# Layer 0 of a two-layer macaron block: who loads x, when the chains run, and how the attention's averages are spread over the next key tile

## The chip, the cores and the metric

The kernel runs on one core of one Trainium2 chip. The metric is the device time of one execution in microseconds; the time of a kernel is the median of its runs. The engines are TensorE (PE in the profile; its weight loads are PEld), VectorE (DVE), ScalarE (ACT), GpSimd (POOL) and SyncE (SP), whose queue issues most transfers. Each engine works through its own list of instructions in the order in which they stand there.

## The reference

Layer 0 works on x, 16 batches of 512 tokens with 128 features: half a quantized feed-forward network is added, then an attention with relative positions, then half a feed-forward network again. Layer 1 (mixture of experts and linear attention) follows and is not touched here.

```python
def _L0_attn_ref(x, W_qkv, b_qkv, W_out, b_out, rel_emb_k, rel_emb_v):
    ...
    dist = jnp.clip(idx[None, :] - idx[:, None], -R, R) + R      # R = 64
    pe_k = rel_emb_k[dist]
    pe_v = rel_emb_v[dist]
    ...
    score = jnp.einsum('bhqd,bhkd->bhqk', q, k) + jnp.einsum('bhqd,qkd->bhqk', q, pe_k)
    attn = jax.nn.softmax(score, axis=-1)
    ctx = jnp.einsum('bhqk,bhkd->bhqd', attn, v) + jnp.einsum('bhqk,qkd->bhqd', attn, pe_v)
    ctx = jnp.transpose(ctx, (0, 2, 1, 3)).reshape(b, s, d)
    return ctx @ W_out + b_out

def _L0_ffn_ref(x, w_gate, w_up, w_down):
    ...                                  # fp4_linear rounds both operands to 4 bits in blocks of 16
    gate = fp4_linear(x, w_gate)
    y = fp4_linear(x, w_up)
    h = jax.nn.silu(gate) * y
    return fp4_linear(h, w_down)
...
x = x + 0.5 * _L0_ffn_ref(_layernorm(x, axis=-1), ...)
x = x + _L0_attn_ref(_layernorm(x, axis=-1), ...)
x = x + 0.5 * _L0_ffn_ref(_layernorm(x, axis=-1), ...)
```

There are 16 heads of 8 features.

## The kernel before

The attention of layer 0 works in 32 units: a unit is half a batch, 256 queries, against all 512 keys of the batch in four key tiles of 128. A score is one PSUM tile of 128 keys by 32 queries of 16 heads: four matmuls of queries and keys (L263) and, where the distances are not clipped, eight more for the relative positions (L267). Every score is computed twice. The first time DVE takes its maximum over the keys (`maxima`, L341; per unit 32 scores, then a reduction `mk` at L347, a transpose on PE at L349, and the negated maxima go by way of MD in HBM into row 28 of the query tile a_BD). The second time the maximum is already in the operands, and ScalarE takes the exponential into PT (`main`, L369). Both kinds of scores share three PSUM buffers (`pS`). The maxima run about half a unit ahead of the exponentials.

With PT, PE computes the averages (`av`, 16 matmuls a key tile) and the band runs for the relative positions of the values (`rps`, 16 or 32 matmuls a run); `run` (L272 to L274) keeps the matmuls of such a run together. ScalarE copies the band sums to RV (L403) and the averages to cx (L412). RV goes to HBM (RD, L406) and comes back in another order (a_cr, L409); `fin` adds it (L422), divides, and applies the output weights (L430, L437, L440, L443).

Besides, there are chains of small steps: `head` is the first feed-forward half of a half batch, `tail` the last (both `FFN.half`: L55 statistics, L62, L116, L121, L123, L126, L133, L139, L140), `prep` makes queries and keys of a batch and writes them to HBM (QS, QM, KSd, L286 to L309), `prepV` the values. `loads` brings a_KS (L315), a_BD (L329) and a_TQ (L330) back for the maxima of a unit. `tail` ends with the store of the half batch (L486).

The tile of x of a batch lives from the load (L475) through head, prep, fin and tail to the second store. Its pool `xk` has five buffers, so batch b takes that of batch b-5. In the kernel before, `head` itself loads x, on SP's queue, when it begins.

`interleave` (L446) sets the order of the program: each generator has a number of steps n and a start f and an end t in units, and the one whose next step is due first goes on. A unit u starts at time u. `main` has 59 steps: eight scores of a key tile, then the averages and four empty steps, then the band runs of a finished half with empty steps. The numbers in W are the due times of the chains, counted from their unit; `pl` and `hl` say how many batches ahead prep and head run. The tile framework then places the instructions on each engine by a simulated timeline, in which this order is the priority, and adds the waits.

Of the kernel before, what the change touches and what calls it, by code (L numbers as in the profile page):

```python
# [8 lines left out]
F32 = mybir.dt.float32  # L9
# [136 lines left out]
class Attn0:  # L146
# [103 lines left out]
    @staticmethod  # L250
    def vers(kt,half):

        return 1 if kt*128+192<half*256+256 else 0
# [12 lines left out]
                w0=kt*128-blk*32-x+a.OFF  # L266
                nc.tensor.matmul(out[:,x*64:x*64+64],a.ET[:,w0:w0+128],TQ[:,:,b*32+4*x:b*32+4*x+4],start=False,stop=(x==7),skip_group_check=True)  # L267

    xnT={}; pend={}; last=None
    def run(a, mms):  # L270

        r=a.nc.tensor.matmul(*mms[0][0],**mms[0][1])  # L272
# [85 lines left out]
    def main(a, b, half, X, wk, big, pS, pA, pM):  # L358
        s=a.s; nc=a.nc; i=b%2
        u=(2*b+half)%3; BD=a.BD[u]; TQ=a.TQ[u]; KS=a.KS[b%2]; V=a.V[b%2]; RD=a.RD[half]; cr=a.cr[0]  # L360
        av=[pA.tile([128,512],F32,name=f"av{z}") for z in range(2)]
        RV=wk.tile([128,4,4,4,16],F32,name="RV")
        PT=[None]*4
        for kt in range(4):
            pt=big.tile([128,16,256],F32,name="PT"); PT[kt]=pt
            for bb in range(8):
                ps=pS.tile([128,512],F32,name="sps")
                a.scores(ps,kt,half,bb,BD,TQ,KS)
                nc.scalar.activation(pt[:,:,bb*32:bb*32+32].rearrange("p h (x j) -> p x h j",j=4),ps.rearrange("p (x h j) -> p x h j",x=8,j=4),AF.Exp)  # L369
                yield  # L370
            vs=a.vers(kt,half)
            mms=[]
            for z in range(4):
                for cg in range(4):
                    h=z*4+cg
                    o=av[z//2][cg*32:cg*32+32,(z%2)*256:(z%2)*256+256]
                    fs=(kt==0 and z%2==0)
                    mms.append(((o,V[:,2*kt-1+vs,h*9:h*9+32],pt[:,h,:]),dict(start=fs,stop=(kt==3),skip_group_check=True,tile_position=(0,cg*32))))
            a.run(mms)
            for _ in range(4): yield  # L380
            for hb in range(2):
                bl=range(hb*4,hb*4+4)
                ks=[k for k in range(4) if any(a.inband(k,half*8+x) for x in bl)]
                if max(ks)!=kt: continue
                rps=pA.tile([128,512],F32,name="rps")
                first=[True]*4
                mms=[]
                for b0 in bl[::2]:
                    ok=[(bb,k) for k in reversed(ks) for bb in (b0+1,b0) if a.inband(k,half*8+bb)]
                    for n,(bb,k) in enumerate(ok):  # L390
                        blk=half*8+bb
                        for x in range(8):
                            cg=x%4; col=(bb-hb*4)*128+(x//4)*64
                            v0=(blk*32-k*128+a.UO)//8
                            mms.append(((rps[cg*32:cg*32+32,col:col+64],a.TV[a.vers(k,half)][:,x,v0-8*a.vers(k,half):v0-8*a.vers(k,half)+4,:].rearrange("p v d -> p (v d)"),
                                PT[k][:,:,bb*32+4*x:bb*32+4*x+4]),
                                dict(start=first[cg],stop=(k==min(q for p,q in ok if p==bb)),skip_group_check=True,tile_position=(0,cg*32))))
                            first[cg]=False
                    a.run(mms); mms=[]
                    yield  # L400
                    yield
                for c in range(4):
                    nc.scalar.copy(RV[:,:,c,:,hb*8:hb*8+8].rearrange("p j z a -> p a z j"),rps.rearrange("p (a z c j) -> p c a z j",a=8,z=4,j=4)[:,c])  # L403
                yield

        nc.sync.dma_start(RD[:,:4*8*1024].rearrange("x (r f) -> x r f",f=1024),RV)  # L406
        for c in range(4):
            src=bass.AP(tensor=RD.tensor,offset=RD.offset+c*64,ap=[[1024,8],[8*1024+256,16],[1,64]])
            nc.sync.dma_start(cr[c*32:c*32+8].rearrange("p (xj f) -> p xj f",f=64),src)  # L409
        cx=wk.tile([128,4,256],F32,name="cx")  # L410
        for zz in range(2):
            nc.scalar.copy(cx[:,2*zz:2*zz+2,:].rearrange("p z (b j x) -> p (z b) x j",j=4,x=8),av[zz].rearrange("p (y x j) -> p y x j",x=8,j=4))  # L412
        a.pend[b,half]=cx,cr
        yield

    def fin(a, b, half, X, wk, pM):

# [28 lines left out]
def interleave(*gens):  # L446

    live=[[g,n,0,f,t] for g,n,f,t in (q if len(q)==4 else (*q,0,1) for q in gens)]
    while live:
        k=min(live,key=lambda r:r[3]+(r[4]-r[3])*r[2]/r[1])  # L450
        try: next(k[0]); k[2]+=1
        except StopIteration: live.remove(k)
# [4 lines left out]
def layer0(tc, s, w, src, dst, nb=16):  # L457
    nc=tc.nc
    tok=lambda x,b: x[b].rearrange("(t p) d -> p t d",p=128)
    P="L0_attn_"; names=["W_qkv","b_qkv","W_out","b_out","rel_emb_k","rel_emb_v"]  # L460
    with ExitStack() as c:
        s.const=c.enter_context(tc.tile_pool(name="c",bufs=1))
        pM=c.enter_context(tc.tile_pool(name="pM",bufs=2,space=PS))
        pF=c.enter_context(tc.tile_pool(name="pF",bufs=0,space=PS)) if 0 else pM
        pS=c.enter_context(tc.tile_pool(name="pS",bufs=3,space=PS))
        pX=pS
        pA=c.enter_context(tc.tile_pool(name="pA",bufs=1,space=PS))
        wk=c.enter_context(tc.tile_pool(name="wk",bufs=1))
        fk=c.enter_context(tc.tile_pool(name="fk",bufs=2))
        xk=c.enter_context(tc.tile_pool(name="xk",bufs=5))  # L470
        X={}
        def xload(b):
            if b in X or b>=nb: return
            t=xk.tile([128,4,128],F32,name="x"); X[b]=t
            nc.sync.dma_start(t,tok(src,b))  # L475
        def head(b,h):

            if b<nb: xload(b); yield from F.half(X[b],h,fk,pF)
        def prep(b):
            if b<nb: yield from A.prep(b,X[b],wk,pM)  # L480
        def prepV(b):
            if b<nb: yield from A.prepV(b,pM)
        def tail(b,h):
            if b<0: return
            yield from F.half(X[b],h,fk,pF)
            nc.sync.dma_start(tok(dst,b)[:,2*h:2*h+2,:],X[b][:,2*h:2*h+2,:])  # L486
        def mxs(b,half):
            if b>=nb: return
            yield from A.maxima(b,half,wk,pX,pM)
        def loads(u):  # L490
            if u<2*nb:
                if u%2==0: A.loadK(u//2)
                A.load(u//2,u%2)
        def stream():
            for u in range(1,2*nb):
                for k,_ in enumerate(mxs(u//2,u%2)):
                    if k==16: loads(u+1)
                    yield
        st=stream()
        def part(n):  # L500
            for _ in range(n):
                if next(st,0)==0: return
                yield
        pl,hl=2,3
        W=dict(part=0,V=(.6,.7),fin=(.45,.9),prep=(0,.7),tail=1.0,head=(-.1,1))
        with tc.tile_pool(name="wp",bufs=1) as wp:
            for b in range(3): xload(b)
            F=FFN(s,w["L0_ffn_w_gate"],w["L0_ffn_w_up"],w["L0_ffn_w_down"],wp,pF)
            ffn2=lambda f,b: interleave((f(b,0),21,0,.8),(f(b,1),21,.2,1))
            ffn2(head,0)  # L510
            A=Attn0(s,wp,pS,*[w[P+n] for n in names])
            def run(g):
                for _ in g: pass
            run(prep(0)); run(prepV(0)); loads(0); run(mxs(0,0))
            FFN1.pre(s,wp,[pA.tile([128,512],F32,name=f"av{z}") for z in range(2)]+[pA.tile([128,512],F32,name="rps")],w)
        big=c.enter_context(tc.tile_pool(name="big",bufs=3))
        loads(1); ffn2(head,1); run(prep(1)); run(part(14)); ffn2(head,2)
        S=[(part(99999),33*2*nb,W['part'],2*nb+W['part'])]
        for b in range(nb):
            for h in range(2):  # L520
                u=2*b+h
                def at(g,n,f,t): S.append((g,n,u+f,u+t))
                at(A.main(b,h,X,wk,big,pS,pA,pM),59,0,1)
                fn,tl=(W['fin'],W['tail']) if u<2*nb-2 else ((.3,.5),.6)
                at(A.fin(b,h,X,wk,pM),5,1+fn[0],1+fn[1])
                at(tail(b,h),21,1+fn[1]+.001,1+fn[1]+tl)
                if b+hl<nb: at(head(b+hl,h),21,*W['head'])
                if h==0 and b+pl<nb: at(prep(b+pl),11,*W['prep'])
                if h==1 and b+1<nb: at(prepV(b+1),1,*W['V'])
        interleave(*S)  # L530


# [249 lines left out]
class Attn1:  # L782
# [38 lines left out]
    X={}  # L821
# [216 lines left out]
```

## Time and profile before

| what | value |
|---|---|
| median of 3 runs | 3630.38 us (3630.13 to 3631.83) |
| profiled execution, its own time | 3633.94 us |
| its span | 3632.2 us |
| loop of layer 0 (first to last exponential) | 175.5 to 1974.5 us |
| PE busy, share of the span | 2825.0 us, 78% |
| DVE busy | 2444.9 us, 67% |
| ACT busy | 1693.8 us, 47% |
| POOL busy | 838.9 us, 23% |

The busy times are sums over stages with different limits, so the loop of layer 0 has to be read by itself. In listings of waits the columns are: the waiting engine, tile and line, what it waited for, the total in us, how many times, the longest in us. In listings in order of time they are start, duration, engine, line, operation, output from input, and in brackets the idle time before with what ended it. In tables of windows they are the stretch, its length, the busy time of PE, PEld, DVE, ACT and POOL with the number of instructions, the granted clock of PE as a share of full speed, the busy share of the DMA engines, and GB/s; a sum line adds up the stretches.

### The profile page before, as it was taken

How to read it: one execution, taken by the hardware profiler on the slowest of the kernel's cores; microseconds unless marked ns; L12 is line 12 of the kernel's file. 1: busy time of each engine (PE TensorE's matmuls, PEld its weight loads, DVE VectorE, ACT ScalarE, POOL GpSimd, SP SyncE). 2: the span in 40 equal slices, each digit the busy share in tenths (PEclk: the TensorE clock that was granted, in tenths of full speed). 3: DMA queues.
4: the chain of work that ended last, by engine and by line, in shares of the span. 5: the costliest groups of instructions: out<-in, count | busy, mean ns of one | idle time of the engine just before them, and what ended most of it. 6: DMA issues, size and time to landing. Idle time of an engine off the chain costs nothing. (4 is left out here: it accounts for less than half of the span.)

```text
span 3632.2 us, 95259 instructions
## 1 busy us (share of the span) xinstructions
PE 2825.0 (78%) x40077; PEld 2032.3 (56%) x40077; DVE 2444.9 (67%) x6508; ACT 1693.8 (47%) x3391; POOL 838.9 (23%) x789
## 2 busy tenths in 40 slices
PE   5578989889898889888896388873788888878570
PEld 3357777667676677666775244431565555555230
DVE  5568788777887788877773467774546655655356
ACT  3145555545455454545554155533455454445242
POOL 4122222222222222222110222212112211111226
PEclk8799999999999999999998599886899989989785
DMA  3232222321223222222210111104312222121401
GB/s 105 54 91 71 57 53 59 81 63 52 65 65 77 64 50 58 76 74 62 53 33 19 32 33 36 36 33 123 90 54 73 59 63 56 36 62 36 126 17 46
DMA packets 290159, 217.23 MB, mean 60 GB/s; under 512 B 77402, under 2 KB 257476, under 8 KB 289604
## 3 DMA queue, kind: packets, MB, share of 16 engines
q1 hardware_dynamic: 284468, 207.72, 21.6%
q8 instruction: 315, 5.16, 0.6%
q10 hardware_dynamic: 5264, 3.43, 0.4%
q14 instruction: 112, 0.92, 0.1%
HBM read 110.28 MB, written 100.78 MB: 58 GB/s over the span
## 5 line engine op out<-in xcount | busy, mean ns | idle before, releaser
L341 DVE TRANSPOSE_TENSOR_REDUCE mx<-sps 128x16 f32<-128x512 f32 x1024 | 702.5, 701 | 261.7 <-PE sps L263 137.2
L263 PE MATMUL sps<-a_BD,a_KS 128*128 128x128 f16 x8192 | 736.4, 222 | 136.2 <-DVE mx L341 65.6
L369 ACT ACTIVATE PT<-sps 128x512 f32<-128x512 f32 x1024 | 576.4, 599 | 433.8 <-PE sps L267 238.1
L263 PEld LDWEIGHTS <-a_KS 128*128 128x128 f16 x8192 | 546.1, 98 | 296.4 <-issue 260.0
L59 POOL TENSOR_TENSOR ln_rs<-ln_ve,negh 128x4 f32<-128x4 f32 (+1 forms) x192 | 176.9, 930 | 855.1 <-DVE ln_ve L58 760.6
L267 PE MATMUL sps<-a_TQ,a_ET 128*128 128x64 f16 x7168 | 370.3, 195 | 0.0
L721 DVE SCALAR_TENSOR_TENSOR moe<-mps,oh,moe 128x128 f32<-128x128 f32 x896 | 289.8, 341 | 110.7 <-PE mps L719 96.5
L79 POOL TENSOR_TENSOR q_M<-q_y,q_M 128x704 f32<-128x704 f32 (+2 forms) x129 | 157.0, 1218 | 784.6 <-DVE q_y L78 658.6
L719 PE MATMUL mps<-f_W,T 128*128 128x512 f32 x512 | 297.1, 701 | 24.8 <-DVE moe L721 20.0
L267 PEld LDWEIGHTS <-a_ET 128*128 128x128 f16 x7168 | 311.2, 99 | 2.3 <-issue 1.9
L274 PE MATMUL av<-PT,a_V 128*32 128x256 f32 x3840 | 251.9, 387 | 0.0
L894 DVE TENSOR_TENSOR a_at<-pp,a_cm 128x1024 f32<-128x1024 f32 x128 | 154.3, 1214 | 79.6 <-PE pp L892 78.6
L892 PE MATMUL pp<-a_F 64*128 64x128 f32 x2048 | 169.8, 306 | 41.4 <-DVE a_at L894 30.2
L892 PEld LDWEIGHTS pp<-a_F 64*128 64x128 f32 x2048 | 143.3, 206 | 93.0 <-DVE a_at L894 36.9
L719 PEld LDWEIGHTS mps<-f_W,T 128*128 128x128 f32 x512 | 102.7, 222 | 125.0 <-issue 75.3
L274 PEld LDWEIGHTS av<-PT,a_V 128*32 128x32 f32 x3840 | 121.4, 111 | 68.7 <-issue 5.0
L874 ACT ACTIVATE a_F<-pp 128x1024 f32<-128x1024 f32 x128 | 127.0, 1025 | 46.8 <-PE pp L872 40.5
L62 ACT ACTIVATE xn<-xn,ln_mr,ln_rs 128x128 f32<-128x128 f32 x256 | 103.6, 481 | 95.5 <-DVE ln_mr L60 75.2
L274 PE MATMUL rps<-PT,a_TV 128*32 128x64 f32 x6912 | 134.5, 222 | 4.6 <-issue 4.4
L139 PE MATMUL mps<-wdT,hT 128*128 128x128 f32 (+1 forms) x768 | 126.9, 301 | 5.6 <-ACT hT L136 4.0
L673 ACT COPY f_PT<-St 32x512 f32<-32x512 f32 x128 | 78.7, 615 | 106.0 <-DVE St L672 99.9
L872 PE MATMUL pp<-a_QK,a_PK 128*128 128x512 f16 x256 | 82.7, 413 | 54.4 <-DMA a_QK<-a1d 26.6
(342 smaller groups left out, 5330.2 us busy)
## 6 DMA issues: line engine op xcount, KB each, us to landing
QM<-a_HM SPq DMA_DIRECT2D x180, 128.0 KB
a_TQ<-QM SPq DMA_DIRECT2D x120, 192.0 KB
RD<-RV SPq DMA_DIRECT2D x32, 512.0 KB
a_KS<-KSd SPq DMA_DIRECT2D x128, 96.0 KB
a_QK<-a1d SPq DMA_DIRECT2D x128, 96.0 KB
xn<-X SPq DMA_DIRECT2D x32, 256.0 KB
a1d<-a_hi SPq DMA_DIRECT2D x64, 128.0 KB
a_BD<-QS SPq DMA_DIRECT2D x128, 58.0 KB
```

Source lines behind the costliest of these rows:

```text
L59: nc.gpsimd.tensor_tensor(rs,ve,s.negh[:,:n],ALU.pow); yield
L79: nc.gpsimd.tensor_tensor(M[:P],y[:P],M[:P],ALU.subtract)
L263: nc.tensor.matmul(o4[:,g],KS[:,sd,g*512+kt*128:g*512+(kt+1)*128],BD[:,g,:,b*32:b*32+32].rearrange("p h (x j) -> p x h j",j=4),start=(g==0 ...
L267: nc.tensor.matmul(out[:,x*64:x*64+64],a.ET[:,w0:w0+128],TQ[:,:,b*32+4*x:b*32+4*x+4],start=False,stop=(x==7),skip_group_check=True)
L274: for p,q in mms[1:]: a.nc.tensor.matmul(*p,**q)
L341: with a.s.tc.high_priority(): r=nc.vector.tensor_reduce(mx[:,kt,:,bb],ps.rearrange("p (i c) -> p i c",c=32),axis=AX.X,op=ALU.max,apply_tr ...
L369: nc.scalar.activation(pt[:,:,bb*32:bb*32+32].rearrange("p h (x j) -> p x h j",j=4),ps.rearrange("p (x h j) -> p x h j",x=8,j=4),AF.Exp)
L719: nc.tensor.matmul(ps,yT[:,j*128:(j+1)*128],a.W[:,e2*4:e2*4+4,:],start=True,stop=True)
L721: nc.vector.scalar_tensor_tensor(moe[:,j,:],ps[:,e*128:(e+1)*128],oh[:,j,e2*4+e:e2*4+e+1],moe[:,j,:],ALU.mult,ALU.add)
L874: nc.scalar.activation(f,ps,AF.Relu)
L892: nc.tensor.matmul(ps[:,hh,bs],f[hh*64:hh*64+64,1,bs],f[hh*64:hh*64+64,0,bs],start=True,stop=True)
L894: nc.vector.tensor_tensor(k,ps.rearrange("p h (b q) -> p (h b) q",b=4),a.cm.unsqueeze(1).to_broadcast([128,8,128]),ALU.mult)
```

## The change

The load of x leaves `head` and becomes a generator of its own, `xl`, issued on ScalarE's queue with a due time 1.3 to 1.4 units before the unit by which it is counted. Head runs two batches ahead instead of three, with later due times; fin, tail and prep are due later as well; the head of batch 2 moves from before the loop into it. `main` has 32 steps, one per score, with no empty ones: averages, band runs, copies and the end of a unit are put into a list `todo`, and after each exponential one portion of the list is issued. A unit's last portions run among the first scores of the next unit; `rest` issues what is left at the very end. The tiles av, rps and RV are allocated when the first portion needs them.

```diff
-    xnT={}; pend={}; last=None
+    xnT={}; pend={}; last=None; todo=[]
...
     def main(a, b, half, X, wk, big, pS, pA, pM):
...
+        def avrun(kt):
+            if kt==0: T["av"]=[pA.tile([128,512],F32,name=f"av{z}") for z in range(2)]
...
+            a.run(mms)
+        def rvrun(hb, b0, ks):
+            if b0%4==0: T["rps"]=pA.tile([128,512],F32,name="rps"); T["first"]=[True]*4
...
+            a.run(mms)
+        def rvcopy(hb):
+            if hb==0: T["RV"]=wk.tile([128,4,4,4,16],F32,name="RV")
+            for c in range(4):
+                nc.scalar.copy(T["RV"][:,:,c,:,hb*8:hb*8+8].rearrange("p j z a -> p a z j"),T["rps"].rearrange("p (a z c j) -> p c a z j",a=8,z=4,j=4)[:,c])
+        def end():
+            nc.sync.dma_start(RD[:,:4*8*1024].rearrange("x (r f) -> x r f",f=1024),T["RV"])
...
+            a.pend[b,half]=cx,cr
         for kt in range(4):
...
                 nc.scalar.activation(pt[:,:,bb*32:bb*32+32].rearrange("p h (x j) -> p x h j",j=4),ps.rearrange("p (x h j) -> p x h j",x=8,j=4),AF.Exp)
+                if a.todo: a.todo.pop(0)()
                 yield
-            a.run(mms)
-            for _ in range(4): yield
+            a.todo.append(lambda kt=kt: avrun(kt))
             for hb in range(2):
...
-                    a.run(mms); mms=[]
-                    yield
-                    yield
...
+                a.todo+=[lambda hb=hb,b0=b0,ks=ks: rvrun(hb,b0,ks) for b0 in bl[::2]]+[lambda hb=hb: rvcopy(hb)]
+            if kt==3: a.todo.append(end)
+    def rest(a):
+        while a.todo: a.todo.pop(0)(); yield
...
-        def xload(b):
-            if b in X or b>=nb: return
+        def xload(b, eng=nc.sync):
             t=xk.tile([128,4,128],F32,name="x"); X[b]=t
-            nc.sync.dma_start(t,tok(src,b))
+            eng.dma_start(t,tok(src,b))
+        def xl(b):
+            xload(b,nc.scalar); yield
         def head(b,h):
-            if b<nb: xload(b); yield from F.half(X[b],h,fk,pF)
+            if b<nb: yield from F.half(X[b],h,fk,pF)
...
-        pl,hl=2,3
-        W=dict(part=0,V=(.6,.7),fin=(.45,.9),prep=(0,.7),tail=1.0,head=(-.1,1))
+        pl,hl=2,2
+        W=dict(part=0,V=(.6,.7),fin=(.6,1.0),prep=(1.03,1.9),tail=1.0,head=(-1.05,0))
...
-        loads(1); ffn2(head,1); run(prep(1)); run(part(14)); ffn2(head,2)
+        loads(1); ffn2(head,1); run(prep(1)); run(part(14))
...
-                def at(g,n,f,t): S.append((g,n,u+f,u+t))
-                at(A.main(b,h,X,wk,big,pS,pA,pM),59,0,1)
+                def at(g,n,f,t): S.append((g,n,max(u+f,0),max(u+t,.5)))
+                at(A.main(b,h,X,wk,big,pS,pA,pM),32,0,1)
...
+                if h==0 and 2<b+hl<nb: at(xl(b+hl),1,-1.4,-1.3)
                 if b+hl<nb: at(head(b+hl,h),21,*W['head'])
...
+        S.append((A.rest(),8,2*nb,2*nb+.15))
         interleave(*S)
```

More of the change, by code (lines that the diff above doesn't have):

```diff
@@ L360, in main @@
         u=(2*b+half)%3; BD=a.BD[u]; TQ=a.TQ[u]; KS=a.KS[b%2]; V=a.V[b%2]; RD=a.RD[half]; cr=a.cr[0]
-        av=[pA.tile([128,512],F32,name=f"av{z}") for z in range(2)]
-        RV=wk.tile([128,4,4,4,16],F32,name="RV")
-        PT=[None]*4
+        PT=[None]*4; T={}; vers=a.vers
+        def avrun(kt):
+            if kt==0: T["av"]=[pA.tile([128,512],F32,name=f"av{z}") for z in range(2)]
+            vs=vers(kt,half)
+            mms=[]
+            for z in range(4):
+                for cg in range(4):
+                    h=z*4+cg
+                    o=T["av"][z//2][cg*32:cg*32+32,(z%2)*256:(z%2)*256+256]
+                    fs=(kt==0 and z%2==0)
+                    mms.append(((o,V[:,2*kt-1+vs,h*9:h*9+32],PT[kt][:,h,:]),dict(start=fs,stop=(kt==3),skip_group_check=True,tile_position=(0,cg*32))))
+            a.run(mms)
@@ new lines, in rvrun @@
+        def rvrun(hb, b0, ks):
+            if b0%4==0: T["rps"]=pA.tile([128,512],F32,name="rps"); T["first"]=[True]*4
+            rps=T["rps"]; first=T["first"]
+            mms=[]
+            ok=[(bb,k) for k in reversed(ks) for bb in (b0+1,b0) if a.inband(k,half*8+bb)]
+            for bb,k in ok:
+                blk=half*8+bb
+                for x in range(8):
+                    cg=x%4; col=(bb-hb*4)*128+(x//4)*64
+                    v0=(blk*32-k*128+a.UO)//8-8*vers(k,half)
+                    mms.append(((rps[cg*32:cg*32+32,col:col+64],a.TV[vers(k,half)][:,x,v0:v0+4,:].rearrange("p v d -> p (v d)"),
+                        PT[k][:,:,bb*32+4*x:bb*32+4*x+4]),
+                        dict(start=first[cg],stop=(k==min(q for p,q in ok if p==bb)),skip_group_check=True,tile_position=(0,cg*32))))
+                    first[cg]=False
+            a.run(mms)
@@ new lines, in rvcopy @@
+        def rvcopy(hb):
[4 more added lines that the diff above has]
+            nc.sync.dma_start(RD[:,:4*8*1024].rearrange("x (r f) -> x r f",f=1024),T["RV"])
+            for c in range(4):
+                src=bass.AP(tensor=RD.tensor,offset=RD.offset+c*64,ap=[[1024,8],[8*1024+256,16],[1,64]])
+                nc.sync.dma_start(cr[c*32:c*32+8].rearrange("p (xj f) -> p xj f",f=64),src)
+            cx=wk.tile([128,4,256],F32,name="cx")
+            for zz in range(2):
+                nc.scalar.copy(cx[:,2*zz:2*zz+2,:].rearrange("p z (b j x) -> p (z b) x j",j=4,x=8),T["av"][zz].rearrange("p (y x j) -> p y x j",x=8,j=4))
+            a.pend[b,half]=cx,cr
@@ L369, in main @@
                 nc.scalar.activation(pt[:,:,bb*32:bb*32+32].rearrange("p h (x j) -> p x h j",j=4),ps.rearrange("p (x h j) -> p x h j",x=8,j=4),AF.Exp)
+                if a.todo: a.todo.pop(0)()
                 yield
[L371 to L378, printed above, removed]
-            a.run(mms)
-            for _ in range(4): yield
+            a.todo.append(lambda kt=kt: avrun(kt))
             for hb in range(2):
@@ L384, in main @@
                 if max(ks)!=kt: continue
[L385 to L398, printed above, removed]
-                    a.run(mms); mms=[]
-                    yield
-                    yield
[L402 to L414, printed above, removed]
+                a.todo+=[lambda hb=hb,b0=b0,ks=ks: rvrun(hb,b0,ks) for b0 in bl[::2]]+[lambda hb=hb: rvcopy(hb)]
+            if kt==3: a.todo.append(end)
+    def rest(a):
+        while a.todo: a.todo.pop(0)(); yield
     def fin(a, b, half, X, wk, pM):
```

## The prediction

> **What bounds the kernel now.** I read the span by slices first, then stretches of it by engine, then who waited for whom, then the order of time around the longest waits. The attention loop of layer 0 runs from the first exponential at 175.5 us to 1975 us, half of the span; the rest is not touched. In the loop:
>
> ```profile
> core 0: us, PE busy (x) PEld busy (x) DVE busy (x) ACT busy (x) POOL busy (x), PEclk, DMA share, GB/s
> 1000.00:1200.00 200.00, 179.77 (x3154) 141.06 (x3152) 163.66 (x364) 105.20 (x232) 48.55 (x47) 0.97 0.26 66
> ```
>
> PE sets the pace: it is busy for 90% at a granted clock of 0.97, DVE for 82%. What can be won is PE's idle tenth and the clock. The list of waits, from 400 to 1800 us, and that of the SP queue, say where it goes:
>
> ```profile
> DVE ln_st L55 <- DMA x<-in_L_attn_x_dram: 45.5, 11, 5.2
> PE sps L263 <- DVE mx L341: 45.0, 53, 3.9
> PE sps L263 <- ACT PT L369: 27.1, 64, 2.6
> PE sps L349 <- DVE hq_sc L71: 9.9, 11, 0.9
> ```
> ```profile
> SPq L475 <- DMA X<-x: 28.8, 11, 3.4
> ```
>
> Eleven times, once per batch (each batch has two units), DVE stands still for a load of x that is issued when it is already needed. The load can't be issued earlier: SP holds it until the store of an older batch has left the buffer. The order of time at one of the eleven:
>
> ```profile
> 756.29 0.39 SPq L486 DMA_DIRECT2D X<-x  x1
> 760.14 0.39 SPq L475 DMA_DIRECT2D x<-in_L_attn_x_dram  x1
> 760.64 1.68 SPq L315 DMA_DIRECT2D a_KS<-KSd  x4
> ...
> 765.24 3.55 SPq L330 DMA_DIRECT2D a_TQ<-QM  x1
> ...
> 774.04 3.36 SPq L330 DMA_DIRECT2D a_TQ<-QM  x1
> 777.50 0.66 SPq L406 DMA_DIRECT2D RD<-RV  x1
> ```
> ```profile
> 763.46 1.07 DVE L55 BATCH_NORM_STATS2 ln_st<-x 128x6 f32<-128x128 f32 x5 [5.16 <-DMA x<-in_L_attn_x_dram]
> ```
> ```profile
> 766.07 0.59 PE L263 MATMUL sps<-a_BD,a_KS 128*128 128x128 f16 x4 [3.89 <-DVE mx L341]
> ```
>
> PE idles 3.89 us behind DVE. The same listing shows two more things for later: a store of x lands 3.5 us after its issue has ended (756.68 to 760.14), and from the last four a_KS loads to the instruction behind the last a_TQ load SP needs 16.9 us (760.64 to 777.50).
>
> **The change part by part.** Line numbers are those of the kernel before. *The wait for x goes.* The windows of 8 us that begin with DVE's eleven waits, and eleven windows of 80 us between them, sum to:
>
> ```profile
> sum 88.00, PE 55.06 PEld 41.12 DVE 42.69 ACT 33.64 POOL 14.82; mean PE 5.01 PEld 3.74 DVE 3.88 ACT 3.06 POOL 1.35
> ```
> ```profile
> sum 880.00, PE 792.97 PEld 603.74 DVE 749.94 ACT 446.38 POOL 201.69; mean PE 72.09 PEld 54.89 DVE 68.18 ACT 40.58 POOL 18.34
> ```
>
> PE idles 32.9 of 88 us around the waits and 9.9% elsewhere, which would be 8.7: 24 us are owed to x. Behind a wait the clock sinks too:
>
> ```profile
> 768.00:770.00 2.00, 2.00 (x29) 2.00 (x28) 2.00 (x7) 1.15 (x4) 0.00 (x0) 0.50 0.21 63
> 770.00:774.00 4.00, 4.00 (x99) 3.86 (x97) 3.16 (x14) 2.28 (x4) 1.10 (x1) 0.78 0.18 47
> ```
>
> With 766 to 768 also at 0.50 the worst wait lost 1.0 + 1.0 + 0.9 = 2.9 us of clock; I take half of that as the mean of the eleven, 16 us (bounds 0 and 32). In the changed program x is loaded about a unit before its first L55, so 24 + 16 = 40 us go (24 to 56).
>
> The Trainium skill speaks of the clock in "TensorE: Matmul & The Clock Gate", section "What's actually happening": half rate comes after about 3.4 us of idling. By that rule alone only the three or so waits over 3.4 us would cost clock, some 9 us by the row of the worst, and the part would be 33 us, not 40. The row decides.
>
> *ScalarE's queue gets the load, and with it the wait.* The load still needs its buffer, and so the store of an older batch. In the built order of the changed program the eleven loads that reuse a buffer (batches 5 to 15) stand in ScalarE's order directly behind the second exponential of units 4, 6, ... 24, and the two copies of L116 and the third exponential behind them. The store they wait for is the second of its batch; SP has it behind the a_KS loads and four pairs of a_BD and a_TQ. The last four a_KS wait for the last score of the unit before. What an engine does with a load that waits is shown at the start, where ScalarE issues some:
>
> ```profile
> 95.84 9.16 ACTq L330 DMA_DIRECT2D a_TQ<-QM  x8
> 105.04 0.37 ACT L116 COPY f_x<-mps 128x256 f32<-128x256 f32 x1 [17.45 <-DMA a_TQ<-QM]
> ```
> ```profile
> 105.47 1.54 PE L121 MATMUL mps<-wguT,f_x 128*128 128x352 f32 x2 [13.89 <-ACT f_x L116]
> ```
>
> It holds all that stands behind, here the same L116 and L121 as there. The price, counted from the last score of unit 2b-1: SP 16.9 us for the loads, 0.4 for the store's issue, 3.5 until it lands, 0.4 for the load's issue, 0.4 for L116: PE can go on with L121 at 21.6 us. Until then PE has, in its order: nine scores at 0.47 us (eight L267 follow four L263 by 0.23 us twice), L133 0.84, two L139 at 0.94, the averages 1.9, two band runs of 16 at 0.33, four L115 0.76: 10.3 us. Idle 11.3, less the 1 us that it would idle anyway in 10: 10.3 us, eleven times: 113. The clock costs what it did behind x, 16: +129. After such a stop DVE and ScalarE have no backlog, so the usual tenth is missing for some 10 us: 1 us each, -11. Bounds: where a_TQ is loaded for a second half batch, three of them go out in 1.34 us (at 700.59), 0.45 each and not 3.5; the quickest a_BD takes 0.26. With such rows SP needs 1.7 + 2.8 + 0.4 + 3.5 = 8.4 us, and PE does not stop at all: 0. With a store issue of 3.57 us (as at 714.26) it is 3.2 us more each: 129 + 35 = 164. I take 129, since all loads behind a_KS show the slow rows.
>
> In "DMA: Bandwidth & Descriptors", section "Issuing engines are not separate DMA queues", the skill says that issuing from another engine saves only the time of the issue. Here that would be 11 x 0.39 us on SP, 4 us, and the sum without both waits would lose the 40 us above as well; no row tells issue time from the wait it carries, so this is left at the rows.
>
> *Averages, band runs and copies, one portion per score.* The same instructions, none more. In the built order exponentials' scores and maxima's scores now alternate almost strictly, where before up to five of one kind follow each other, and each portion stands alone. Of PE's 45.0 + 27.1 us behind DVE and ScalarE 24 are x; the other 48 may halve: -24, for the whole loop -30. The chain waits of L437 and L440 (19.4 and 11.4 us before them) get a score or two more cover: -20. Against it L349, which waits 0.9 us for DVE in eleven units: it now stands one score behind the last maximum in even units, while the reduction (0.70) and both mk (1.06) have to run: about 1 us more in each of 31 units, +30. Together -20 (bounds -60 and +40).
>
> *Chains a unit later.* Preparing a batch now ends just before its loads: twelve QM issues (8.0 us on SP) stand ahead of MD and the a_BD row it feeds. From the order I count seven pairs of scores, 12 us, between that row and the next unit: 0; without that cover the first score would wait. RD goes behind the same slow loads: 16.9 + 0.4, then 9.6 until a_cr is issued (SP waits 9.6 at most for RD), 1.4 and some 2.5 to land: 31 us after the boundary, and its sum (L422) stands 19 pairs behind, about 34: 0. The head of batch 2 moves from before the loop into it, and so the last head a unit later: 6.5 us of PE work for each half, gone at the start and back at the end: 0 (10 either way).
>
> The sum, from the profiled execution's own 3633.9 (span 3632.2 and 1.7 around it): - 40 + 129 - 11 - 20 = 3692. The median of the runs is 3.6 lower: **3688 us**.
>
> **The rivals.** *The store lands in time* (faster): the loads go out as fast as the half-unit rows, or ScalarE reaches its load later than I count. Then only the gains are left: 3634 - 40 - 20, less 4 to the median, 3570 (3545 to 3600). It decides wherever the store lands within 10 us of the last score. For it: fast a_TQ rows exist. Against: SP's 16.9 us recur behind every a_KS group. Chance 0.15. *Half covered*: PE has 5 us more to do than counted; +65 in place of +129: about 3624. Chance 0.09. *RD takes over*: ScalarE goes free, but L422 comes to wait for a_cr on DVE, at 3.7 us for 14 batches, +52: 3622; for it the margin of only 3 us, against it that before no wait of that kind is in the list. 0.05. *More of it*: the slow store issue, or the alternation costing: 3720 to 3780. 0.09. The forecast itself: 0.62, 3640 to 3720.
>
> **How the numbers follow.** A measurement of this kernel tells 0.2% (7 us) from no change. Faster: 0.15 + 0.03 of the half covered + 0.02 of RD = 0.20. Same: 0.03 + 0.03 = 0.06. Slower: 0.62 + 0.09 + 0.03 = 0.74. The range, 3605 to 3765, leaves out the first rival and the top of the fourth, under 0.2; for the forecast alone it is 3640 to 3720.
>
> **What would show it.** Right: in the changed profile DVE no longer waits for x at L55; ScalarE idles 10 to 12 us eleven times before L116, put down to the store of x or its load, with SP's a_TQ issues in the same stretch; PE's L121 waits as long for L116; the clock in the loop stays below 0.98. PE's scores wait less for DVE and ScalarE elsewhere, L349 more. Wrong: ScalarE passes its x load without idling (then 3570), or a_TQ behind a_KS is issued in under 1 us, or DVE waits at L422.

## The result and the profile after

The changed kernel takes 3823.09 us (median of 4 runs, 3820.93 to 3828.05) against 3630.26 us (4 runs, 3623.89 to 3631.83): 1.0537 times the time before, 95% interval 1.0518 to 1.0555. It is slower by 193 us; 3688 us had been forecast, 58 us slower. The profiled execution took 3828.05 us, its span is 3826.3 us.

Where the time went shows first in the starts of the units, taken as the first exponential of each. From unit 4 to unit 26 the kernel before takes 1270.1 us, 115.5 us for a pair of units (a batch); the changed one takes 1466.9 us, 133.4 us. These eleven batches are 197 us longer; the spans differ by 194. Outside them, the first exponential comes 4 us later, the first four units are 16 us quicker, the last six 23 us slower, and what follows the loop is 14 us shorter; together these take off only 3 us. The head of batch 2 and the later chains have moved to the two ends; how much of these shifts is theirs was not taken apart. Within a pair the odd unit is nearly as before (59.0 against 58.2 us); the even one takes 74.4 us instead of 57.2.

The window that was shown of before (1000 to 1200 us), in the changed kernel: stretch and length, then busy time and instructions of each engine, granted clock, DMA share, GB/s.

```profile
core 0: us, PE busy (x) PEld busy (x) DVE busy (x) ACT busy (x) POOL busy (x), PEclk, DMA share, GB/s
1000.00:1200.00 200.00, 164.89 (x2703) 129.72 (x2702) 147.36 (x320) 93.24 (x198) 46.83 (x42) 0.90 0.24 59
```

PE falls from 179.8 to 164.9 us, its clock from 0.97 to 0.90. The list of who waited for whom, from 400 to 1800 us (total, times, longest):

```profile
PE mps L121 <- ACT f_x L116: 144.6, 11, 13.4
PE sps L263 <- ACT PT L407: 45.1, 110, 0.7
PE sps L349 <- DVE mk L347: 27.4, 13, 2.3
PE sps L263 <- DVE mx L341: 20.9, 44, 1.1
PE mps L434 <- DVE cx L426: 20.0, 20, 2.8
PE mps L125 <- DVE f_h L123: 18.1, 11, 2.8
...
DVE ln_st L55 <- DMA x<-in_L_attn_x_dram: 203.1, 11, 20.0
...
ACT f_x L116 <- DMA X<-x: 153.2, 11, 14.2
```

Eleven times PE stands still for 13 us before L121, as forecast in kind and number. The line that was not forecast is DVE's: it still waits for x at L55, eleven times, and four times as long as before (203.1 against 45.5 us). The order of time at one of the eleven, from the listings of SP, ScalarE, DVE and PE (start, duration, instruction, in brackets the idle time before it and what ended it):

```profile
540.06 1.55 SPq L315 DMA_DIRECT2D a_KS<-KSd  x4
...
544.42 3.32 SPq L330 DMA_DIRECT2D a_TQ<-QM  x1
...
553.07 3.54 SPq L330 DMA_DIRECT2D a_TQ<-QM  x1
556.70 0.69 SPq L491 DMA_DIRECT2D X<-x  x1
557.50 0.55 SPq L394 DMA_DIRECT2D RD<-RV  x1
568.21 1.36 SPq L397 DMA_DIRECT2D a_cr<-RD  x4
...
547.10 1.06 ACT L391 COPY RV<-rps 128x128 f32<-128x128 f32 x4 [0.24 <-PE rps L274]
561.86 0.40 ACTq L478 DMA_DIRECT2D x<-in_L_attn_x_dram  x1
562.30 0.65 ACT L116 COPY f_x<-mps 128x256 f32<-128x256 f32 x2 [14.14 <-DMA X<-x]
...
548.36 0.72 DVE L341 TRANSPOSE_TENSOR_REDUCE mx<-sps 128x16 f32<-128x512 f32 x1 [1.15 <-PE sps L263]
569.03 0.49 DVE L55 BATCH_NORM_STATS2 ln_st<-x 128x6 f32<-128x128 f32 x2 [19.95 <-DMA x<-in_L_attn_x_dram]
...
562.73 2.71 PE L121 MATMUL mps<-wguT,f_x 128*128 128x352 f32 x4 [13.35 <-ACT f_x L116]
570.41 1.54 PE L125 MATMUL mps<-wguT,f_x 128*128 128x352 f32 x2 [2.80 <-DVE f_h L123]
```

Both ScalarE and DVE run into the same late store. SP has the store behind a_KS and a_TQ and issues it at 556.70, where DVE's last L140 on that x had ended at 545.7 (a row not shown). ScalarE reaches the load at 548.2 and is held until 561.86; L116 and PE's L121 stand behind it. DVE reaches L55 of the very x that is being loaded at 549.1, and is held until 569.03: the load lands 6.8 us after its issue has ended (2.9 us in the listing of before), and RD, 512 KB issued at 557.50 and read back only at 568.21, is in flight beside it. This is the longest of the eleven; the others take 5.2 to 5.6 us (before: 2.7 to 4.6, 3.1 in the mean). The clock at that place:

```profile
551.00:553.00 2.00, 0.00 (x0) 0.00 (x0) 0.00 (x0) 0.00 (x0) 0.00 (x0) 1.00 0.09 25
553.00:555.00 2.00, 0.00 (x0) 0.00 (x0) 0.00 (x0) 0.00 (x0) 0.00 (x0) 0.59 0.39 100
...
563.00:565.00 2.00, 2.00 (x4) 1.05 (x5) 0.00 (x0) 1.40 (x3) 0.00 (x0) 0.50 0.58 166
...
567.00:569.00 2.00, 0.61 (x15) 0.49 (x12) 0.00 (x0) 0.60 (x1) 0.00 (x0) 1.00 0.08 27
569.00:571.00 2.00, 0.59 (x1) 0.50 (x2) 1.55 (x8) 0.00 (x0) 0.70 (x1) 0.86 0.29 66
571.00:573.00 2.00, 2.00 (x18) 1.40 (x17) 1.97 (x4) 0.16 (x1) 0.00 (x0) 0.50 0.00 0
```

PE comes back at half rate, gets the full rate just when it stops again behind DVE, and pays a second time at 571 us; seven of the eleven places show such a second stretch. Adding up PE's busy time at half rate over 411 to 1800 us and halving it gives 82.0 us lost to the clock, 7.9 a batch; in the kernel before it is 29.8 us, 2.5 a batch. PE's idle time goes from 13.1 to 28.0 us a batch by the same count. Idle time and clock together make 20.3 us a batch, 2.4 more than the 17.9 by which a pair is longer; by the same count PE's work at full rate is 2.4 us less (the ends of matmuls are modelled).

### The profile page after: what moved, and what is told of

The parts are those of the page before. It is cut to its first block, busy times and chain, and to the rows that moved or that the text cites. A ratio compares the mean times of both kernels' runs of the same rounds, so it can differ in the third digit from the quotient of the medians.

```text
span 3826.3 us, 95189 instructions
## 1 busy us (share of the span) xinstructions
PE 2865.8 (75%) x40077; PEld 2076.7 (54%) x40077; DVE 2475.2 (65%) x6508; ACT 1721.3 (45%) x3391; POOL 848.9 (22%) x789
## 5 line engine op out<-in xcount | busy, mean ns | idle before, releaser
L407 ACT ACTIVATE PT<-sps 128x512 f32<-128x512 f32 x1024 | 603.1, 600 | 714.9 <-PE sps L267 380.7
L263 PE MATMUL sps<-a_BD,a_KS 128*128 128x128 f16 x8192 | 763.6, 226 | 152.3 <-ACT PT L407 71.0
L263 PEld LDWEIGHTS <-a_KS 128*128 128x128 f16 x8192 | 571.9, 101 | 332.3 <-issue 302.1
L267 PE MATMUL sps<-a_TQ,a_ET 128*128 128x64 f16 x7168 | 381.3, 196 | 0.0
L267 PEld LDWEIGHTS <-a_ET 128*128 128x128 f16 x7168 | 321.7, 100 | 2.3 <-issue 1.2
L79 POOL TENSOR_TENSOR q_M<-q_y,q_M 128x704 f32<-128x704 f32 (+2 forms) x129 | 168.7, 1312 | 680.8 <-PE sps L267 298.9
L121 PE MATMUL mps<-wguT,f_x 128*128 128x352 f32 x256 | 118.8, 561 | 160.1 <-ACT f_x L116 159.3
L55 DVE BATCH_NORM_STATS2 ln_st<-x 128x6 f32<-128x128 f32 x192 | 47.2, 274 | 204.3 <-DMA x<-in_L_attn_x_dram 203.1
L121 PEld LDWEIGHTS mps<-wguT,f_x 128*128 128x128 f32 x256 | 47.4, 220 | 174.1 <-ACT f_x L116 161.9
```

The lines of the kernel that those rows point to most:

```text
L79: nc.gpsimd.tensor_tensor(M[:P],y[:P],M[:P],ALU.subtract)
L121: nc.tensor.matmul(g[:,:I],xqT[:,j*128:(j+1)*128],f.wguT[:,0,:],start=True,stop=True)
L263: nc.tensor.matmul(o4[:,g],KS[:,sd,g*512+kt*128:g*512+(kt+1)*128],BD[:,g,:,b*32:b*32+32].rearrange("p h (x j) -> p x h j",j=4),start=(g==0 ...
```

## The experiments

Twelve runs. Each ratio is to the kernel before on the same chip; the medians of before lay between 3622 and 3644 us, so ratios are compared, not medians. "A pair" is the mean length of a batch between units 4 and 26 of the profiled execution: 115.5 us before, 133.4 us changed.

**Who issues the load.** In the changed kernel only the queue of the load is changed. PE, DVE and ScalarE keep their order.

```diff
-            xload(b,nc.scalar); yield
+            xload(b,nc.sync); yield
```

> The changed kernel with the load of x issued by SP again; the order on PE, DVE and ScalarE is the same instruction for instruction, on SP the load stands directly behind the store it waits for. Theory A (what costs is that ScalarE is held): the 13 us stops of PE go, 11 x 16 us, about 3640. Theory B (x is late for DVE whoever loads it, because its buffer comes free only when a store behind SP's slow a_TQ loads has landed): ScalarE no longer idles, PE runs some 8 us on, then stops behind DVE at L55; x lands earlier than now because RD is not in flight beside it; 8 us a batch less, 3735 (3700 to 3770), and DVE's wait for x at L55 stays over 10 us eleven times. Theory C (portions and the later chains cost by themselves): within 30 us of 3823.

Measured: 3811.66 us, ratio 1.0473 (1.0448 to 1.0498); a pair takes 130.6 us. In its list of waits, 400 to 1800 us:

```profile
PE mps L125 <- DVE f_h L123: 151.8, 11, 14.5
...
DVE ln_st L55 <- DMA x<-in_L_attn_x_dram: 170.5, 11, 16.2
```

With ScalarE free, PE gets through L121 and some scores and stops 13.8 us before L125 instead, behind DVE. Theory A falls, and B's 8 us a batch were too many: 2.8 came. Before L125, which waits for DVE, PE had only L121 and three scores more to do, 2.9 us (546.76 to 549.61 in that run's listing of PE), and the gain is of that size.

**An earlier store.** The stores of x go to GpSimd's queue, the load stays on ScalarE.

```diff
-            nc.sync.dma_start(tok(dst,b)[:,2*h:2*h+2,:],X[b][:,2*h:2*h+2,:])
+            nc.gpsimd.dma_start(tok(dst,b)[:,2*h:2*h+2,:],X[b][:,2*h:2*h+2,:])
```

> The changed kernel with the stores of x issued by GpSimd, so that they no longer stand behind SP's loads. The load stays on ScalarE (two L116 ahead of it now). Theories A and B agree: the store goes out right after L140, lands some 13 us earlier, ScalarE idles under 4 us, DVE waits 3 to 5 us for x as in the kernel before, and 11 x 14 us go: 3670 (3640 to 3700). Theory C: the stops go but the time stays over 3720.

Measured: 3730.65 us, ratio 1.0259 (1.0229 to 1.0289); a pair takes 123.8 us. The listing of ScalarE and the list of waits:

```profile
547.54 0.40 ACTq L478 DMA_DIRECT2D x<-in_L_attn_x_dram  x1
547.99 1.09 ACT L407 ACTIVATE PT<-sps 128x512 f32<-128x512 f32 x2 [4.13 <-DMA X<-x]
...
DVE ln_st L55 <- DMA x<-in_L_attn_x_dram: 105.7, 11, 9.9
...
PE mps L125 <- DVE f_h L123: 47.6, 11, 5.2
```

Only the time of the store was moved, and more than half of the loss is gone: what counts is when the store lands. ScalarE waits 4.1 us as expected, but DVE 9.6 us and not 3 to 5, since the load again takes 6 us to land. Here RD is issued 5 to 7 us after the load, in two of the eleven only when the load has landed, so RD is not what delays it; SP's last a_TQ goes out at that time. That the time missed 3640 to 3700 is put down to this longer wait.

**Holding ScalarE without DVE.** x is loaded in halves, into five fixed tiles, so that the half that L55 needs waits only for the older half's own store.

```diff
+        XT=[xk.tile([128,4,128],F32,name=f"x{i}") for i in range(5)]; X={}
...
+        def xhalf(b, h, eng):
+            X[b]=XT[b%5]
+            eng.dma_start(X[b][:,2*h:2*h+2,:],tok(src,b)[:,2*h:2*h+2,:])
+        def xl(b, eng=nc.scalar):
+            xhalf(b,0,eng); yield
+            xhalf(b,1,eng); yield
...
-                if h==0 and 2<b+hl<nb: at(xl(b+hl),1,-1.4,-1.3)
+                if h==0 and 2<b+hl<nb: at(xl(b+hl),2,-1.4,-.4)
```

> The changed kernel with x loaded in two halves into five fixed tiles: each half waits only for the store of its own half. Both loads stay on ScalarE. In the built order the second half's load stands where the whole load stood, behind the second exponential of even units, and still waits for the late store; the first half's, the only one that L55 needs there, comes a unit earlier. So DVE is free of the wait and ScalarE is held as before. Theory B alone (only DVE's wait for x counts): 3650. Theory D (the late store holds two engines side by side, ScalarE and DVE, and either is enough to stop PE): PE's L121 still waits 12 to 13 us for L116 eleven times, 3800 (3770 to 3820).

Measured: 3934.89 us, ratio 1.0866 (1.0845 to 1.0887). DVE no longer waits for x; PE does all the same. From the list of waits:

```profile
PE sps L263 <- ACT PT L407: 145.6, 88, 17.2
PE mps L121 <- ACT f_x L116: 119.2, 9, 13.7
...
ACT f_x L116 <- DMA X<-x: 126.1, 9, 14.5
ACT PT L407 <- DMA X<-x: 120.4, 10, 15.4
```

The expectation had missed that the first half's load is also put right behind its store: ScalarE is now held in odd units too, which take 69.3 us and not 59.0. D's mechanism stands, its number does not.

**Holding neither.** The same halves on SP (`xl(b, eng=nc.sync)`).

> The same two half loads, issued by SP: neither ScalarE nor DVE waits for the second store. Theories B and D: the stop of 13.7 us and its clock go from eleven even units, all units near 58 us, 3640 (3610 to 3670); what is then left over the kernel before is what portions and later chains cost. Theory C (those cost 100 us or more): over 3720.

Measured: 3710.37 us, ratio 1.0240 (1.0221 to 1.0259); a pair takes 122.5 us. No wait for x at L55, none at L116. But 7.8 us of idle PE are left in each batch, behind a wait that did not show before. List of waits, then the listing of SP and ScalarE:

```profile
PE sps L263 <- ACT PT L407: 134.0, 124, 8.8
...
ACT RV L391 <- DMA RD<-RV: 91.2, 12, 9.0
```
```profile
550.33 0.69 SPq L495 DMA_DIRECT2D X<-x  x1
555.40 0.40 SPq L481 DMA_DIRECT2D x<-in_L_attn_x_dram  x1
555.90 0.54 SPq L394 DMA_DIRECT2D RD<-RV  x1
...
565.95 1.01 ACT L391 COPY RV<-rps 128x128 f32<-128x128 f32 x4 [7.97 <-DMA RD<-RV]
```

RV has one buffer. Its next copies must wait until RD has read it, and RD goes out on SP behind a_TQ, the store and the load. In the changed kernel the stop for x had covered this.

**RD off SP, then the stores too.** Both on top of the halves on SP.

```diff
-            nc.sync.dma_start(RD[:,:4*8*1024].rearrange("x (r f) -> x r f",f=1024),T["RV"])
+            nc.scalar.dma_start(RD[:,:4*8*1024].rearrange("x (r f) -> x r f",f=1024),T["RV"])
```

> The changed kernel with the two half loads of x on SP, and RD issued by ScalarE right behind the RV copies it stores; nothing else. Theory E (the 7.8 us that PE stood still behind L407 with the half loads were ScalarE's RV copies waiting until RD, late on SP, had read the buffer): that gap goes, 11 x 8 us and some clock, 3615 (3590 to 3640). If the gap is something else it stays, 3700 to 3720.

> The same, and the stores of x issued by GpSimd as well, so that SP waits neither for RV copies nor for a landed store. Theory E: SP's waits of 4 us for the store go, which nothing on PE waited for: 3610 (3585 to 3640), the changed kernel's portions and later chains without any of its late transfers. If it is then at or under the kernel before, these parts by themselves cost nothing; if it stays over 3680, theory C is right for the rest.

Measured: with RD on ScalarE 3652.22 us, ratio 1.0071 (1.0047 to 1.0094), a pair 117.8 us. The 7.8 us are gone. The expected range, 3590 to 3640, was missed by 12 us; what shows in their place is a wait of 4 us on ScalarE around the issue of RD, put down to a_TQ:

```profile
537.27 0.53 ACTq L394 DMA_DIRECT2D RD<-RV  x1
537.85 1.08 ACT L407 ACTIVATE PT<-sps 128x512 f32<-128x512 f32 x2 [4.06 <-DMA a_TQ<-QM]
```

With the stores on GpSimd as well 3602.32 us, ratio 0.9932 (0.9906 to 0.9957), a pair 113.3 us: this version is 0.7% faster than the kernel before, and theory C falls: portions and later chains, here with x in halves, cost nothing on the whole once no transfer is late. The window of 1000 to 1200 us is nearly that of before again:

```profile
1000.00:1200.00 200.00, 178.03 (x3137) 142.35 (x3126) 165.83 (x372) 104.76 (x221) 54.85 (x50) 0.95 0.26 64
```

**The two moves on the kernel before.** RD on ScalarE and the stores on GpSimd in the kernel before, nothing else.

> The kernel before with RD issued by ScalarE and the stores of x by GpSimd; x is loaded by SP as before, without SP's wait of 2.6 us for the store. Theory E: DVE's wait for x (4.1 us, eleven times) shrinks by about half, RD and a_cr come up to 8 us earlier, which nothing waited for: 3610 (3590 to 3630). If issuing on ScalarE and GpSimd costs more than it frees: 3640 or more.

Measured: 3611.11 us, ratio 0.9954 (0.9937 to 0.9971). DVE's wait for x only went from 45.5 to 39.3 us, less than expected. Against this base the portions, the later chains and x in halves, with all late transfers removed, are worth 0.2%, and the two intervals overlap. The starts of the units in the profiled executions show more: the two moves alone do not shorten a pair (116.0 us, 115.5 before), their gain lies at the ends of the loop and behind it. With the rest of the change a pair is 2.7 us shorter (113.3), 29 us on eleven, and most of that is lost again from unit 26 to the last exponential (291.4 against 271.4 us).

**The portions alone.** The changed `main` with the old times of the chains and the old load of x (first run), and the same with RD on ScalarE and the stores on GpSimd (second).

```diff
...
-        pl,hl=2,2
-        W=dict(part=0,V=(.6,.7),fin=(.6,1.0),prep=(1.03,1.9),tail=1.0,head=(-1.05,0))
+        pl,hl=2,3
+        W=dict(part=0,V=(.6,.7),fin=(.45,.9),prep=(0,.7),tail=1.0,head=(-.1,1))
...
```

> The kernel before with averages, band runs and copies in portions, and nothing else: old times of the chains, x loaded by SP in the head. Theories A and B (portions are worth what the prediction gave them, -20, bounds -60 and +40): 3610 (3570 to 3670). Theory C: over 3700.

> The portions alone (old times of the chains, whole loads of x by SP) with RD issued by ScalarE and the stores of x by GpSimd. In the run of portions alone PE stood still some 5 us in every batch behind DVE at L307, which waited for the QS and KSd stores that SP had behind RD and a_cr. If that lateness is what the portions cost, RD and a_cr now come earlier and the 5 us mostly go: 3615 (3595 to 3640), level with the kernel before under the same two moves (3611). If the portions cost by themselves (their order, the slower clock): 3650 or more.

Measured: 3676.76 us, ratio 1.0107 (1.0068 to 1.0146); with the moves 3632.75 us, ratio 0.9971 (0.9956 to 0.9987). The list of waits of the first:

```profile
PE mps L434 <- DVE qklo L307: 53.4, 11, 6.0
...
DVE qklo L307 <- DMA QS<-qkhi: 56.3, 12, 6.8
```

Alone, the portions make the kernel 1.1% slower: PE stops 5 us a batch behind L307, whose buffer waits for a store that SP has behind RD and a_cr. The expectation of the second run was half right: the time is back, but the wait at L307 is not gone (49.1 us, 11 times). SP's listings, the first run's and then the second's, show what both have in common: twelve stores of QM stand between a_cr and that store of QS (issued at 462.68 and 458.63), and the two moves leave them there.

```profile
451.40 9.25 SPq L300 DMA_DIRECT2D QM<-a_HM  x12
```
```profile
447.51 9.06 SPq L300 DMA_DIRECT2D QM<-a_HM  x12
```

What gave the time back was not taken apart.

**The later chains alone.** The changed kernel with the old `main`.

> The changed kernel with the old main (averages and band runs between the key tiles as before): only the load of x on ScalarE and the later chains are left of the change. In its built order SP has the store of x behind RD and the four a_cr loads, which wait 10 us for RD, so it lands later still, and the load stands three scores later on ScalarE. Theories A and B: ScalarE idles 15 us or more eleven times, 3840 (3800 to 3900). Theory C, if the portions are what costs: under 3700.

Measured: 3847.24 us, ratio 1.0579 (1.0551 to 1.0607). ScalarE is held for 198.0 us, 11 times, 18 each: the store stands behind a_cr and lands later still. The stop does not need the portions. The late chains and the load on ScalarE were both left in, and the load on ScalarE under the old due times was not run, so the share of the chains is not shown.

**x in halves in the kernel before.** Each head loads its own half on SP.

```diff
...
-            if b<nb: xload(b); yield from F.half(X[b],h,fk,pF)
+            if b<nb: xhalf(b,h); yield from F.half(X[b],h,fk,pF)
```

> The kernel before with x loaded in two halves by SP at the start of each head, nothing else: the wait that the change was priced to remove, by itself. The prediction gave it 40 us (24 to 56): 3595 (3580 to 3615). If the wait is covered by what is queued in front of PE, or DVE's backlog shifts it elsewhere: within 15 us of before.

Measured: 3912.55 us, ratio 1.0794 (1.0774 to 1.0815). It does not answer what the wait was worth; the built order puts the second half's load behind a_TQ, with the L55 that needs it long due. Listing of SP, list of waits:

```profile
581.10 3.42 SPq L330 DMA_DIRECT2D a_TQ<-QM  x1
584.56 0.74 SPq L478 DMA_DIRECT2D x<-in_L_attn_x_dram  x1
...
DVE ln_st L55 <- DMA x<-in_L_attn_x_dram: 246.7, 20, 16.1
```

It shows something else: with neither ScalarE's load nor the portions nor the later chains in it, the kernel before becomes 290 us longer when x is late at L55 twenty times.

**Is it SP's issuing?** The a_TQ loads go to GpSimd's queue, in the changed kernel.

```diff
-            (nc.sync if b else nc.scalar).dma_start(TQ[j*32:j*32+24], ...)
+            (nc.gpsimd if b else nc.scalar).dma_start(TQ[j*32:j*32+24], ...)
```

> The changed kernel, its a_TQ loads of batches 1 to 15 issued by GpSimd; on SP the store of x then stands behind a_KS and four a_BD only. Theory E (all that stands behind the last score of a unit on SP is late by SP's 15 us of a_TQ issues, and the store and load of x, RD and what follows inherit it): store and load of x some 12 us earlier, PE's stop at L121 under 4 us, 3680 (3640 to 3720). Rival F (it is the transfers, not SP's issuing: the packets of a_TQ fill the DMA engines, and a small store or load among them lands late from any queue): the stop stays over 8 us, over 3760.

Measured: 3803.95 us, ratio 1.0493 (1.0462 to 1.0525). The listing of SP and GpSimd, then the list of waits:

```profile
539.00 11.48 SPq L315 DMA_DIRECT2D a_KS<-KSd  x8
550.52 12.06 SPq L329 DMA_DIRECT2D a_BD<-QS  x4
562.68 2.95 SPq L491 DMA_DIRECT2D X<-x  x1
...
549.44 2.92 POOL L330 DMA_DIRECT2D a_TQ<-QM  x4 [3.18 <-PE sps L263]
```
```profile
ACT RV L391 <- DMA X<-x: 150.8, 10, 16.0
```

E's reading of SP falls, the rival F holds as far as the time goes: the stop stays, with ScalarE now held 15 us before the copies into RV instead of before L116. GpSimd needs 0.7 us for an issue of a_TQ, but SP now needs 3 us for each a_BD, which took 0.3 to 1.0 us at the same place of the changed kernel, and 3 us for the store, which took 0.7. From the last a_KS to the end of the store's issue it is 15 us, against 16 in the changed kernel. So the slow issues on SP are not the price of issuing a_TQ. What they wait for is open: the 16 DMA engines are busy for a mean share of 0.28 only from 541 to 557 us of the changed kernel, and the trace does not tell the share of each. Where another queue carries the store itself (the run with stores on GpSimd), it lands 6 us after its issue.

## Why the forecast was half right

The direction and the place were right, the size was not: 58 us forecast, 193 measured. By its own steps:

- *ScalarE's queue gets the wait: +113 of idle PE.* Right in mechanism. From the last four a_KS (540.06) to L116 (562.30) it took 22.2 us where 21.6 were counted; PE's work until then was a little less than counted, and the stop 13.1 us where 11.3 were counted (10.3 after the usual idle time was taken off): 144.6 instead of 124, or 113. The store took 4.5 us to land and not 3.5. The relief behind the stop, -11, did not come: in the 10 us behind it, where the forecast had no idle time, PE idles 1.9 us in the mean, most of it at L125 behind DVE.
- *The wait for x goes: -40.* This is the step that failed. The forecast took x as loaded about a unit before its first L55. By due times the load stands only a third of a unit ahead of the head (1.4 against 1.05), and in the run nothing of it is left: in DVE's order L55 stands three maxima behind the last L140 on the older x, and DVE reaches it at 549.1, 0.9 us after ScalarE reaches the load and 12.8 us before the load is issued. The wait stayed, 18.5 us long, mostly beside ScalarE's stop, and added 18.1 us of idle PE at L125. The runs with the load on SP and with halves on ScalarE show that each of the two held engines stops PE by itself for about the same time (13.8 and 13.2 us), so that freeing ScalarE alone gave 0.6% of the time before, and freeing both (halves on SP) 3.0%. The run that freed DVE alone was 3.3% slower, because it also held ScalarE in the odd units; its even units were 2.0 us shorter.
- *The clock costs what it did behind x: +16, against -16.* Wrong by size, and by 59 us on eleven batches the largest single miss: 2.5 us a batch became 7.9. The stop is long enough for half rate to last 13.7 us, 4 of them after PE has come back, and the second, short stop behind DVE costs another stretch in seven of eleven.
- *Portions, -20.* The wait before L437 and L440 did go (30.6 us before, 2.5 us now, at L441), but that of the step ahead of them grew from 7.1 (L430) to 20.0 us (L434), so that some 15 us were won; L349 waits 27.4 us instead of 15.9, a third of the 30 forecast. That scores would wait half as long for DVE and ScalarE did not come: 66.0 us against 48 without x. Alone the portions cost 1.1%, with RD and the stores moved they are level.
- *RD a queue later: 0.* L426 does not wait for a_cr, as reckoned. But something else waits for RD, the next copies into RV, which the forecast did not look at; 7.8 us a batch lie there, hidden behind the larger stop. *QM ahead of MD: 0* held: no wait of PE for a_BD is in the list. *The head of batch 2: 0* held as a sum: all that lies outside units 4 to 26 comes to 3 us, as said above.

The rule of the Trainium skill that was set against the trace ("DMA: Bandwidth & Descriptors", section "Issuing engines are not separate DMA queues") would make such moves worth the time of the issue alone. Measured, RD and the stores on other queues than SP took the ratio from 1.0240 to 0.9932: in this kernel a queue's order carries waits, and these outweigh the issue of 0.5 us.

What stays open: what the wait for x is worth in the kernel before (no run removed it cleanly), what the loads behind a_KS wait for on SP, and what makes a load of x land late.

## What to carry to other kernels

A load into a reused buffer waits for the store that frees it; give that store a place in its queue that is early enough before moving the load to an engine that computes, or the load will stop that engine. Check in the built order of every engine, not in due times, where the first reader of a loaded tile stands: two engines held by one late transfer hide each other, and freeing one of them shows almost nothing. After a stop is removed look for what it covered, here a single buffer whose store to HBM was equally late.

## What the runs showed of the hardware

The granted clock changes, in the trace's records, only in steps of 3.41 us. PE stopped at 549.4 us, and the rate halved at 553.36; PE resumed at 562.73 and got the full rate at 567.01. At 570.43 it was halved again, after a stretch of 3.41 us in which PE had been busy for some 0.6 us: full idleness is not needed. "TensorE: Matmul & The Clock Gate", section "What's actually happening", has such a free-running window of about 3.4 us and speaks of an idle window; the rows agree with the window, and show that one with a fifth of its time busy counted as idle.

A load of x of 256 KB landed 3.1 us after its issue in the kernel before (mean of eleven), 2.5 us when SP issued it right behind its store with RD behind it (the run with the load on SP), 5.5 us when ScalarE issued it 4 us after SP had issued RD (the changed kernel), and 6.0 us when ScalarE issued it beside SP's a_TQ loads (the run with the stores on GpSimd). What lay in flight before it differs in all four; which of it delays the load was not tested. Slow issues on one queue passed from one kind of load to the next when the first kind was taken away (three a_TQ of 3.3 to 3.5 us each, then four a_BD of 3.0 us each in the mean).
